# A graph product in seven block products, spread over four bursts of a batch, with k and v moved to the batch's end

## The chip, the cores and the metric

The kernel runs on one core of one Trainium2 chip. The metric is the time of one execution on the device in microseconds (us); lower is better. Engines are named as the profile names them: PE is TensorE (its weight loads apart as PEld), DVE is VectorE, ACT is ScalarE, POOL is GpSimd, SP is SyncE, which here only issues DMAs.

## What is computed

Two graph layers over x of shape (16, 1024, 256), f32. The change lies in the first, which makes its queries from a product with a weighted graph (g below) and then does attention with four heads of 64:

```python
fea = transpose(x, (0, 2, 1))                     # (b, 256, 1024)
c_adj = mean(fea, axis=1)
diff = c_adj[:, None, :] - c_adj[:, :, None]
A = abs(abs(sigmoid(diff) - 0.5) - 0.5) * 2.0
A_s = (A + transpose(A, (0, 2, 1))) * 0.5
Wg = adj[None] * A_s                              # (b, 1024, 1024)
g = relu(einsum('bcn,bnm->bcm', fea, Wg) * para)
q = heads(transpose(g, (0, 2, 1)))
k, v = heads(x @ kv_w)
out = softmax(q @ k.T * scale) @ v
x = layernorm(x + out)
# second layer: A_hat @ x, two linear layers with batch norms, residual, layernorm
```

## The kernel before

The kernel has two paths; `fast_path` is what runs (the other is taken if a denominator leaves its range). It goes through three stages: attention for all 16 batches, then aggregation and the first linear layer, then the second linear layer and the final normalisation. The change touches the first.

**Tiles.** A batch's x is a tile of 128 partitions x 8 chunks x 256 (three buffers, pool xp). Its transpose is xT (one buffer, pool xTp). The weighted graph is eight tiles wg of 128x1024, one for each chunk of rows (pool wgp, eight buffers, so the next batch's weights take the buffers as the graph product frees them). q, k and v of a batch are SBUF tiles with two buffers. PSUM has three pools: s (two tiles of 128x1024, for scores), t (two of 128x512, for everything short: transposes, k, v, graph product, denominators) and o (two of 128x512, the attention outputs).

**Order.** PE, ACT and DVE run in the order in which the code records the instructions (`manual_schedule`); each engine is a queue. POOL and SP instructions start when their inputs and buffers are there and the one ahead in their queue is done. The main loop goes over bursts. A batch has 32 units (2 pairs of heads x 2 halves of queries x 8 chunks of keys), a burst is 2 units, so a batch has 16 bursts, u = 0 to 15. In burst u the code records: the scores of its two units and the exps of them on ACT (`scores`); the outputs of the two units of the burst before and, on DVE, the addition of the exps to acc (`outputs`, L931 and L933); then extra work that u selects. The exps p have four buffers, so the exps of a burst wait for the acc additions of the burst two before.

**Extra work, before.** Denominators (`normalise`): after the last burst of a head pair, in bursts 8 and 0 of the next, four matmuls of acc with ones (den), an ACT copy, four DMAs to DRAM and four back. `residual`: four bursts later (12 and 4), per half of queries a reciprocal, four transposes, a product on DVE and an addition to x on POOL (L979). `finish_x1`: in burst 5, statistics and normalisation on DVE (`layernorm`), then a DMA on POOL's queue that stores x; the next x is loaded into the freed buffer.

For the next batch: bursts 10 and 12 transpose x, with the row means (`begin`) ahead of the first; the means go to DRAM and come back as crow, a row on all partitions. Weights (abs and tanh on ACT, a product with adj on DVE, L793) run in bursts 13 to 15 and 0 to 4. k and v (eight steps) run in bursts 0 and 4. The graph product runs in bursts 6, 8, 10 and 12: 32 matmuls of 128x128 by 128x512 in four groups of eight, each group in one t tile, followed by a product with para and the negative scale on DVE and a relu on ACT (`queries`). In the profile each f32 matmul stands as two records, so 960 records at L805 are 480 matmuls in 15 batches. Batch 0 does its own graph product chunk by chunk before the loop (`graph_first`), with k and v of batches 0 and 1 around it.

**Elsewhere.** `left_sums` and `right_sums` (L658 to L669) and `products` (L604) are the seven-product scheme that the second stage already uses.

Of the kernel before, what the change touches and what calls it, by code (L numbers as in the profile page):

```python
# [515 lines left out]
def fast_path(  # L516
# [74 lines left out]
    def layernorm(t, name):  # L591
        st = small.tile([P, NCH, 6], F32, tag="ln_st", name=f"st_{name}")
        mv = small.tile([P, NCH, 2], F32, tag="ln_mv", name=f"mv_{name}")
        rstd = small.tile([P, NCH], F32, tag="ln_rs", name=f"rs_{name}")
        for n in range(NCH):
            nc.vector.bn_stats(st[:, n, :], t[:, n, :])
            nc.vector.bn_aggr(mv[:, n, :], st[:, n, :])
        rsqrt(rstd, mv[:, :, 1], EPS)
        for n in range(NCH):
            nc.vector.tensor_scalar(  # L600
                t[:, n, :], t[:, n, :], mv[:, n, 0:1], rstd[:, n : n + 1], ALU.subtract, ALU.mult
            )

# [96 lines left out]
    with (  # L700
        tc.tile_pool(name="l0c", bufs=1) as l0c,
        tc.tile_pool(name="qkv", bufs=2) as qkv,
# [30 lines left out]
        def prologue(b):  # L733


            s = st[b]
            xt = s["x"]
            first, steps, side = [], [], []

            def step(f, *a):  # L740
                steps.append((f, a))
# [16 lines left out]
            def transpose_x(c, half):  # L758
                if c == 0 and half == 0 and b:
                    begin()  # L760
# [7 lines left out]
                nc.vector.tensor_copy(s["xT"][:, c, half * HALF : (half + 1) * HALF], pt)  # L768
# [28 lines left out]
            def graph_mm(c, half, part):  # L797
                if part == 0:
                    s["pg"] = tile_t(f"pg_{b}_{c}_{half}")
                    if c == 0 and half == 0:  # L800
                        s["qT"] = qkv.tile([P, CC, N], F32, tag="qT", name=f"qT_{b}")
                ps = s["pg"]
                hs = slice(half * HALF, (half + 1) * HALF)
                for n in (2 * part, 2 * part + 1):
                    nc.tensor.matmul(  # L805
                        ps, xt[:, n, c * P : (c + 1) * P], s["wg", n][:, hs],
                        start=(n == 0), stop=(n == NCH - 1),
                    )
                if part == 3:
                    queries(c, hs, ps)  # L810

            def queries(c, hs, ps):
                q = s["qT"][:, c, hs]
                nc.vector.scalar_tensor_tensor(  # L814
                    q, ps, -scale, para_s[:, c, hs], op0=ALU.mult, op1=ALU.mult
                )
                nc.scalar.activation(q, q, AF.Relu)  # L817

            def graph_first(n):

                if n == 0:
                    both = tile_s("pg_0_0")
                    s["pg"] = [both[:, H0], both[:, H1], tile_o("pg_0_1_0"), tile_o("pg_0_1_1")]
                    s["qT"] = qkv.tile([P, CC, N], F32, tag="qT", name="qT_0")
# [6 lines left out]
                if n == NCH - 1:  # L831
                    for c in range(CC):
                        for half, hs in enumerate((H0, H1)):
                            queries(c, hs, s["pg"][2 * c + half])

            def keys(kc, half):
                if kc == 0 and half == 0:
                    s["kT"] = qkv.tile([P, CC, N], F32, tag="kT", name=f"kT_{b}")
# [7 lines left out]
                nc.scalar.copy(s["kT"][:, kc, hs], ps)  # L846

            def values(pair):
                if pair == 0:
                    s["v"] = qkv.tile([P, NCH, C], F32, tag="v", name=f"v_{b}")  # L850
                pt = tile_t(f"pv_{b}_{pair}")
                for j in range(2):
# [6 lines left out]
                nc.vector.tensor_copy(  # L859
                    s["v"][:, 2 * pair : 2 * pair + 2, :].rearrange("p n c -> p (n c)"), pt  # L860
                )

            for i in range(2 * CC):
                first.append((transpose_x, (i // 2, i % 2) if b else (i % 2, i // 2)))
            if b == 0:
                first += [(begin, ()), (row_of_means, ())]
            for i in range(4):
                step(values, i)
                step(keys, i // 2, i % 2)
            for c in range(CC):  # L870
                for half in range(2):
                    for part in range(4):
                        if b:
                            step(graph_mm, c, half, part)
            for n in range(NCH if b == 0 else 0):
                step(graph_first, n)
            for n in range(NCH):
                side.append((weights_abs, (n,)))
                side.append((weights_tanh, (n,)))
                if n:  # L880
                    side.append((weights_adj, (n - 1,)))
            side.append((weights_adj, (NCH - 1,)))
            return first, steps, side
# [11 lines left out]
        def scores(i):  # L895
            b, pr, qh, m = units[i]
            qT, kT = st[b]["qT"], st[b]["kT"]
            ps = tile_s(f"ps_{i}")
            for kh in range(2):
                for hd in range(2):  # L900
# [3 lines left out]
                        ps[kh * D : (kh + 1) * D, hd * HALF : (hd + 1) * HALF], kT[r, pr, ks],  # L904
                        qT[r, pr, qh * HALF : (qh + 1) * HALF], start=True, stop=True,
# [34 lines left out]
        def normalise(b, pr):  # L940
# [10 lines left out]
            row = rdp.tile([P, HALF], F32, tag="drow", name=f"drow_{k}")  # L951
# [28 lines left out]

        def finish_x1(b):
            xt = st.pop(b)["x"]
            layernorm(xt, f"l0_{b}")
# [602 lines left out]
```

## Time and profile before

| | |
|---|---|
| median of 3 runs | 2651.31 us (2650.74 to 2654.38) |
| the profiled execution | 2653.06 us, span in the profile 2651.3 us |
| mean granted PE clock | 0.981 |
| graph product, L805 | 425.2 us busy in 960 records |
| scores, L903, and outputs, L924 | 490.6 and 485.3 us busy |
| k, L842, and v, L855 | 120.3 and 124.0 us busy |
| exps, L908 (ACT) | 495.7 us busy in 512, 1020 ns each |
| acc, L933 and L931 (DVE) | 483.2 and 78.0 us busy |

A busy time is the time in which at least one instruction of the group ran, so a long group of overlapping matmuls counts once. The mean of one instruction goes from its start to its end; successive instructions on ACT and DVE overlap by about 0.1 us, so the distance between starts is the better price in a sum. The span is from the first to the last instruction of the profiled execution; the execution's own time has 1.8 us around it.

### The profile page before, as it was taken

Reading aid. Unit: us, or ns where it says so; the run is one execution under the profiler, and the core shown is the slowest. Engines: PE = TensorE matmul, PEld = TensorE weight load, DVE = VectorE, ACT = ScalarE, POOL = GpSimd, SP = SyncE. Lnnn points to the kernel's source line nnn. Section 1 sums busy time; section 2 is a strip of 40 time slices with the busy share of each in tenths; the row PEclk is TensorE's granted clock in tenths of the full one; section 3 lists DMA queues with packets and bytes.
Section 4 is the critical chain, followed back from the end, with each engine's and each line's share of the span. In section 5 each row is a group of like instructions: output and inputs, shape, how many; then the busy total and the mean of one; then the engine's idle time right before and its main releaser. Section 6 shows DMA issues by size and latency. Waiting matters only on the chain. (4 is left out here: it accounts for less than half of the span.)

```text
span 2651.3 us, 31994 instructions
## 1 busy us (share of the span) xinstructions
PE 2553.7 (96%) x12966; PEld 1110.1 (42%) x12966; DVE 1600.2 (60%) x2160; ACT 1126.8 (43%) x1349; POOL 336.2 (13%) x407
## 2 busy tenths in 40 slices
PE   8999999999999999999999999999999999999964
PEld 4443444444434434444444343344444444444443
DVE  5465665756656657666566576765655655533376
ACT  5363563654645636545446354410101001233368
POOL 0001000100100011001000100321222211100044
PEclk9999999999999999999999999999999999999975
DMA  4001101001011011010110110112122122353367
GB/s 143 2 9 41 33 10 41 21 22 33 9 41 33 9 41 33 10 41 3 39 33 9 41 49 1 41 64 95 80 95 95 66 92 82 137 202 143 149 222 240
DMA packets 134557, 168.94 MB, mean 64 GB/s; under 512 B 86785, under 2 KB 120065, under 8 KB 124033
## 3 DMA queue, kind: packets, MB, share of 16 engines
q1 hardware_dynamic: 129568, 116.47, 14.2%
q0 software_dynamic: 4832, 50.34, 4.6%
q8 instruction: 103, 1.69, 0.3%
q14 instruction: 54, 0.43, 0.0%
HBM read 99.36 MB, written 67.44 MB: 63 GB/s over the span
## 5 line engine op out<-in xcount | busy, mean ns | idle before, releaser
L908 ACT ACTIVATE p<-ps 128x1024 f32<-128x1024 f32 x512 | 495.7, 1020 | 179.5 <-PE ps L903 142.9
L933 DVE TENSOR_TENSOR acc<-acc,p 128x1024 f32<-128x1024 f32 x384 | 483.2, 1258 | 61.0 <-ACT p L908 32.4
L903 PE MATMUL ps<-qT,kT 64*64 64x512 f32 x4096 | 490.6, 594 | 1.4 <-ACT p L908 1.4
L924 PE MATMUL po<-p,v 64*64 64x512 f32 x4096 | 485.3, 589 | 0.0
L805 PE MATMUL pg<-wg,x 128*128 128x512 f32 x960 | 425.2, 596 | 0.0
L979 POOL TENSOR_TENSOR x<-x,o 128x512 f32<-128x512 f32 x64 | 109.5, 1711 | 1434.8 <-DVE o L974 1434.8
L924 PEld LDWEIGHTS po<-p,v 64*64 64x64 f32 x4096 | 156.7, 133 | 282.8 <-issue 282.6
L805 PEld LDWEIGHTS pg<-wg,x 128*128 128x128 f32 x960 | 177.6, 190 | 226.9 <-issue 203.3
L903 PEld LDWEIGHTS ps<-qT,kT 64*64 64x64 f32 x4096 | 146.1, 132 | 280.2 <-issue 231.5
L817 ACT ACTIVATE qT<-qT 128x512 f32<-128x512 f32 x64 | 40.3, 631 | 482.0 <-DVE qT L814 481.9
L1456 PE MATMUL po<-hl,w12T 128*128 128x512 f32 x512 | 220.3, 592 | 3.1 <-ACT hl L1387 2.3
L814 DVE SCALAR_TENSOR_TENSOR qT<-pg,para_s 128x512 f32<-128x512 f32 x64 | 43.9, 689 | 271.1 <-PE pg L805 269.8
L793 DVE SCALAR_TENSOR_TENSOR wg<-wg,adj_s 128x1024 f32<-128x1024 f32 x128 | 153.1, 1217 | 15.5 <-ACT wg L789 15.5
L784 ACT ACTIVATE wg<-crow,ccol 128x1024 f32<-128x1024 f32 x128 | 146.6, 1146 | 11.8 <-DMA crow<-c 11.8
L1456 PEld LDWEIGHTS po<-hl,w12T 128*128 128x128 f32 x512 | 97.1, 190 | 126.3 <-issue 120.5
L789 ACT ACTIVATE wg<-wg 128x1024 f32<-128x1024 f32 x128 | 135.5, 1060 | 2.6
L1387 ACT ACTIVATE hl<-hl,bn_sh,bn_sg 128x1024 f32<-128x1024 f32 x64 | 74.3, 1229 | 135.0 <-DMA hl<-h 133.6
L855 PE MATMUL pv<-kvw_s,xT 128*128 128x256 f32 x512 | 124.0, 385 | 1.6 <-ACT kT L846 1.6
L1460 DVE TENSOR_SCALAR o<-po,col_b 128x1024 f32<-128x1024 f32 x32 | 41.1, 1284 | 139.1 <-PE po L1456 139.1
L842 PE MATMUL pk<-xT,kvw_s 128*128 128x512 f32 x256 | 120.3, 592 | 0.0
L855 PEld LDWEIGHTS pv<-kvw_s,xT 128*128 128x128 f32 x512 | 94.9, 190 | 51.9 <-issue 27.6
L1286 PE MATMUL a_agg<-ahT,x1l 128*128 128x512 f32 x240 | 108.1, 593 | 1.1 <-ACT agg L1104 1.1
(151 smaller groups left out, 2625.4 us busy)
## 6 DMA issues: line engine op xcount, KB each, us to landing
h<-hw POOLq DMA_DIRECT2D x16, 2048.0 KB, 6.6
hl<-h SPq DMA_DIRECT2D x15, 2048.0 KB
x<-x POOLq DMA_DIRECT2D x16, 1024.0 KB, 4.2
x1l<-x SPq DMA_DIRECT2D x16, 1024.0 KB
xf<-x SPq DMA_DIRECT2D x16, 1024.0 KB
out_dram<-o SPq DMA_DIRECT2D x16, 1024.0 KB
x<-in_x_dram SPq DMA_DIRECT2D x15, 1024.0 KB
crow<-c SPq DMA_DIRECT2D x15, 512.0 KB
```

The source lines that it names most:

```text
L784: nc.scalar.activation(w, s["crow"], AF.Abs, bias=s["ccol"][:, n : n + 1])
L789: nc.scalar.activation(w, w, AF.Tanh, scale=0.5)
L793: nc.vector.scalar_tensor_tensor(w, w, 1.0, adj_s[:, n, :], op0=ALU.subtract, op1=ALU.mult)
L805: nc.tensor.matmul(ps, xt[:, n, c * P : (c + 1) * P], s["wg", n][:, hs], start=(n == 0), stop=(n == NCH - 1),)
L842: nc.tensor.matmul(ps, kvw_s[:, c, kc * P : (kc + 1) * P], s["xT"][:, c, hs], start=(c == 0), stop=(c == CC - 1),)
L855: nc.tensor.matmul(pt[:, j * C : (j + 1) * C], s["xT"][:, c, n * P : (n + 1) * P], kvw_s[:, c, C : 2 * C], start=(c == 0), stop=(c == CC - 1),
L903: nc.tensor.matmul(ps[kh * D : (kh + 1) * D, hd * HALF : (hd + 1) * HALF], kT[r, pr, ks], qT[r, pr, qh * HALF : (qh + 1) * HALF], start=Tr ...
L908: nc.scalar.activation(p, ps, AF.Exp)
L924: nc.tensor.matmul(g["po"][kh][hd * D : (hd + 1) * D, :], s["v"][r, m, h * D : (h + 1) * D], p[r, hd * HALF : (hd + 1) * HALF], start=(m = ...
L933: nc.vector.tensor_add(g["acc"], g["acc"], p)
L979: nc.gpsimd.tensor_tensor(xs, xs, o.rearrange("p n h d -> p n (h d)"), ALU.add)
L1456: nc.tensor.matmul(ps[:, hs], w2T[:, k, c * P : (c + 1) * P], h[k][:, hs], start=(k == 0), stop=(k == HC - 1),)
```

## The change

The graph product of batches 1 to 15 is done as a 2x2 block product in seven block products of four matmuls each (28 matmuls instead of 32), each in a t tile of its own. It needs four sums of blocks of x (`left`, on POOL, in the buffer that xT has) and four differences of blocks of wg (`right_first` to `right_fourth`, 16 DVE subtractions of 128x512; two in new tiles t1 and t2, two in place in wg). The products are put together in q by DVE additions out of PSUM, multiplied with para on POOL, and scaled inside the relu.

The order of a batch's bursts changes with it. The next batch's weights run in bursts 11 to 15 and 0, the differences in 0 to 3 and 5 to 7, the block products in bursts 4 (one), 6, 8 and 10 (two each), the transposes of x at the end of 10, and k and v in bursts 12 and 14, after the graph product. `begin` moves to burst 8. Some copies of xT and v go from DVE to ACT, and the layer norm's application goes from DVE to ACT (`statistics_x1` in burst 4, `finish_x1` in burst 5). The residual of the second head pair moves from burst 4 to 3. q and k get a tile per head pair (three buffers each), the denominator row shares a buffer with o, the weights of the second stage are loaded in burst 1 of the last batch instead of burst 6 of the one before, and the statistics tiles of the batch norms move to other pools.

```diff
     def layernorm(t, name):
+        nmr = small.tile([P, NCH], F32, tag="ln_nm", name=f"nm_{name}")
+        def statistics():
             for n in range(NCH):
                 nc.vector.bn_stats(st[:, n, :], t[:, n, :])
                 nc.vector.bn_aggr(mv[:, n, :], st[:, n, :])
             rsqrt(rstd, mv[:, :, 1], EPS)
+            nc.gpsimd.tensor_tensor(nmr, mv[:, :, 0], rstd, ALU.mult)
+            nc.gpsimd.tensor_scalar(nmr, nmr, -1.0, None, ALU.mult)
-        for n in range(NCH):
-            nc.vector.tensor_scalar(
-                t[:, n, :], t[:, n, :], mv[:, n, 0:1], rstd[:, n : n + 1], ALU.subtract, ALU.mult
+        def apply(n):
+            nc.scalar.activation(
+                t[:, n, :], t[:, n, :], AF.Identity,
+                bias=nmr[:, n : n + 1], scale=rstd[:, n : n + 1],
             )
...
             def transpose_x(c, half):
...
+                copy = nc.scalar.copy if half and b else nc.vector.tensor_copy
...
+            LOW = NCH // 2
+            def right_first(i):
...
+                nc.vector.tensor_sub(S["t1"][:, i, :], w[:, H1], w[:, H0])
+            def right_second(i):
+                nc.vector.tensor_sub(S["t2"][:, i, :], s["wg", i + LOW][:, H1], S["t1"][:, i, :])
+            def right_third(i):
+                w = s["wg", i][:, H1]
+                nc.vector.tensor_sub(w, s["wg", i + LOW][:, H1], w)
+            def right_fourth(i):
+                nc.vector.tensor_sub(
+                    s["wg", i][:, H0], s["wg", i + LOW][:, H0], S["t2"][:, i, :]
+                )
+            def left(k):
+                if k == 0:
+                    S["l"] = xTp.tile([P, 4, LOW, P], F32, tag="xT", name=f"xS_{b}")
...
+                nc.gpsimd.tensor_tensor(l[k], one, two, op)
+            def product(k):
+                ps = tile_t(f"pg_{b}_{k}")
+                w = [s["wg", i] for i in range(NCH)]
+                for i in range(LOW):
...
+                        1: lambda: (xt[:, i, C0], w[i][:, H0]),
+                        2: lambda: (xt[:, i + LOW, C0], w[i + LOW][:, H0]),
+                        3: lambda: (S["l"][:, 3, i, :], w[i + LOW][:, H1]),
+                        4: lambda: (xt[:, i + LOW, C1], w[i][:, H0]),
+                        5: lambda: (S["l"][:, 0, i, :], S["t1"][:, i, :]),
+                        6: lambda: (S["l"][:, 1, i, :], S["t2"][:, i, :]),
+                        7: lambda: (S["l"][:, 2, i, :], w[i][:, H1]),
...
+                    nc.tensor.matmul(ps, one, two, start=(i == 0), stop=(i == LOW - 1))
...
+            def times_para(c, half):
...
+                nc.gpsimd.tensor_tensor(q, q, para_s[:, c, hs], ALU.mult)
+            def graph(k):
...
+                if k == 1:
+                    nc.scalar.copy(a, ps)
+                if k == 6:
+                    nc.vector.tensor_add(u, ps, a)
+                if k == 2:
+                    nc.vector.tensor_add(a, ps, a)
+                    times_para(0, 0)
...
+                if k == 7:
+                    nc.vector.tensor_add(v, ps, u)
+                if k == 4:
+                    nc.vector.tensor_add(low, ps, v)
+                    times_para(1, 0)
+                if k == 5:
+                    nc.vector.tensor_add(u, ps, u)
+                    nc.vector.tensor_add(v, ps, v)
+                    times_para(1, 1)
+                if k == 3:
+                    nc.vector.tensor_add(u, ps, u)
+                    times_para(0, 1)
+            def query_last(c, half):
...
+                nc.scalar.activation(q, q, AF.Relu, scale=-scale)
...
             def values(pair):
...
+                copy = nc.scalar.copy if pair % 2 and b else nc.vector.tensor_copy
...
+                "kv": [
+                    (values, (0,)), (keys, (0, 0)), (values, (1,)), (keys, (0, 1)),
+                    (values, (2,)), (values, (3,)), (keys, (1, 0)), (keys, (1, 1)),
+                ],
+                "graph": [(graph, (k,)) for k in (1, 6, 2, 7, 4, 5, 3)],
+                "relu": [(query_last, q) for q in ((0, 0), (1, 0), (1, 1), (0, 1))],
...
+            for i in range(LOW):
+                for n in (i, i + LOW):
+                    side += [(weights_abs, (n,)), (weights_tanh, (n,)), (weights_adj, (n,))]
+                todo["sums"] += [(f, (i,)) for f in (right_first, right_second)]
+            todo["sums"] += [(f, (i,)) for f in (right_third, right_fourth) for i in range(LOW)]
...
-            row = rdp.tile([P, HALF], F32, tag="drow", name=f"drow_{k}")
+            row = rdp.tile([P, HALF], F32, tag="o", name=f"drow_{k}")
...
+                    wait = 5 if j == len(bursts) - 1 or pr == 0 else 4
                     for q in range(2):
-                        full.setdefault(j + 5, []).append((residual, (b, pr, q)))
+                        full.setdefault(j + wait, []).append((residual, (b, pr, q)))
                     if pr == PAIRS - 1:
+                        late.setdefault(j + 5, []).append((statistics_x1, (b,)))
                         late.setdefault(j + 6, []).append((finish_x1, (b,)))
...
+                todo = nxt if b + 1 < B else {}
+                if u == 0 or u == 1:
+                    part("left", 2)
+                part("side", {0: 3, 1: 99}.get(u, 0))
+                part("sums", {0: 2, 1: 2, 2: 2, 3: 2, 5: 4}.get(u, 0))
+                if u == 4:
+                    part("graph", 1)
+                elif u == 6:
+                    part("graph", 2)
+                    part("sums", 2)
+                elif u == 7:
+                    part("relu", 1)
+                    part("sums", 2)
+                elif u == 8:
+                    run(after.get("begin", []), 1)
+                    part("graph", 2)
+                elif u == 10:
+                    part("graph", 2)
+                    part("xT", 4)
+                elif u == 11:
+                    part("relu", 3)
+                if u in (12, 14):
+                    for i in range(4):
+                        part("kv", 1)
+                        run(after["side"], 1 + i % 2)
+                elif u > 10:
+                    run(after["side"], 3)
+                run(full.get(j, []), 9)
...
                 run(sums.get(j, []), 9)
```

In the loop, `nxt` is the batch after the one whose attention runs and `after` the one behind it: the weights of `after` start in burst 11, and at the next burst 0 `after` becomes `nxt`. What burst u's line `run(sums.get(j, []), 9)` records is `normalise`, the last thing of the burst.

## The prediction

> **What bounds the kernel now.** I read the page's first two parts, then the windows through the attention stage (roughly 75 to 1708 us), then the timelines of the engines over one batch (800 to 912 us).
>
> ```profile
> PE 2553.7 (96%) x12966; PEld 1110.1 (42%) x12966; DVE 1600.2 (60%) x2160; ACT 1126.8 (43%) x1349; POOL 336.2 (13%) x407
> ...
> 460.00:560.00 100.00, 99.41 (x648) 41.49 (x650) 64.01 (x85) 52.53 (x60) 9.42 (x7) 1.00 0.09 23
> ...
> L805 PE MATMUL pg<-wg,x 128*128 128x512 f32 x960 | 425.2, 596 | 0.0
> ```
>
> The second line is one stretch of the windows: length, then busy time of PE, weight loads, DVE, ACT and POOL, and the granted clock. TensorE works 99.4 us of every 100 at full clock; DVE is busy 64, ACT 53, POOL 9. Any matmul removed is time gained, as long as no wait replaces it. TensorE has next to none: two of 0.24 and 0.35 us in a batch. A batch takes 104.9 us (the denominator sums of two batches start at 802.43 and 907.33). Why there are no waits is seen where a batch hands over to the next (start, length, engine, line, operation, count):
>
> ```profile
> 895.50 1.92 ACT L908 ACTIVATE p<-ps 128x1024 f32<-128x1024 f32 x2
> ...
> 897.08 2.55 DVE L933 TENSOR_TENSOR acc<-acc,p 128x1024 f32<-128x1024 f32 x2
> ...
> 898.42 1.90 PE L924 MATMUL po<-p,v 64*64 64x512 f32 x16
> 900.25 1.99 PE L855 MATMUL pv<-kvw_s,xT 128*128 128x256 f32 x8
> 902.08 1.88 PE L842 MATMUL pk<-xT,kvw_s 128*128 128x512 f32 x4
> 903.79 1.89 PE L855 MATMUL pv<-kvw_s,xT 128*128 128x256 f32 x8
> 905.52 1.88 PE L842 MATMUL pk<-xT,kvw_s 128*128 128x512 f32 x4
> 907.33 1.07 PE L946 MATMUL den<-acc,ones 128*32 128x512 f32 x8
> ```
>
> den needs the two acc additions of burst 15. They end at 899.6; TensorE reaches den at 907.3, because 7.1 us of k and v stand ahead of it. Last, DVE beside POOL:
>
> ```profile
> 888.61 1.22 DVE L931 TENSOR_TENSOR acc<-p,p 128x1024 f32<-128x1024 f32 x1
> 889.93 2.12 DVE L933 TENSOR_TENSOR acc<-acc,p 128x1024 f32<-128x1024 f32 x1
> ...
> 888.77 2.19 POOL L979 TENSOR_TENSOR x<-x,o 128x512 f32<-128x512 f32 x1 [0.81 <-DVE o L974]
> ...
> 1893.85 1.70 POOL L661 TENSOR_TENSOR x1S<-x1l 128x512 f32<-128x512 f32 x1
> ...
> 1894.47 1.64 DVE L667 TENSOR_TENSOR tT<-agg,tT 128x512 f32<-128x512 f32 x1
> ```
>
> The POOL addition, 1.26 us alone, takes 2.19 beside an acc; the next acc takes 2.12 instead of 1.22. They take turns, a whole instruction each.
>
> [...]
>
> **The change part by part.** Times between starts: eight f32 matmuls 6.87 us (862.43 to 869.30), a burst of two units 3.43, a k or v step 1.75, exp pair 1.82, abs+tanh 2.16 (0.96 the tanh), ACT copy 0.5, adj 1.13, acc 1.23, 128x512 DVE operation 0.61 to 0.69, POOL 128x512 alone 1.26.
>
> *Removed.* 28 matmuls in place of 32, for 15 batches: 4 x 0.859 x 15 = 51.5 us of TensorE.
>
> *Added work, per batch.* DVE: 16 subtractions and 3 operations more on products, 19 x 0.69 = 13.1; away go 4 copies (2.8) and 8 normalisations (8 x 0.407 = 3.3); +7.0. ACT: 5 copies and 8 normalisations, 5 x 0.58 + 8 x 0.504 (row L1526, the same form) = +6.9. POOL: 4 left sums, 4 products with para, 8 x 1.26 = +10.1. Totals (about 71, 60, 19 of 100) fit; these cost nothing by their sums, only by their places.
>
> *den without cover (the main term).* Burst 0 now has no k and v; TensorE goes from outputs straight to den. The weights of the next batch run from burst 11: two in each of bursts 12 and 14, one in 11, 13, 15, 0. Count from TensorE's start of burst 15, which is the end of the last k step of burst 14. ACT: copies that k to 0.6, then tanh (weight 6) to 1.55, exp pair to 3.4, abs and tanh (weight 3) to 5.55. DVE in order: adj of weight 6 from 1.75 to 2.9, two acc of burst 14 to 5.35, adj of weight 3 from 5.65 to 6.8, two acc of burst 15 to 9.3. TensorE: two bursts to 6.9, the half of den that needs only the older acc to 7.45, then waits to 9.4: 2.0 us, bare. But the left sums write the tile that xT had, so POOL may start them when the last k step ends, at 0.15, not in burst 0 where they stand. Four in a row: the first ends at 1.4, the second at 2.65; adj of weight 6 waits 0.9 for it; the third and fourth go in between the next DVE operations, 1.25 each. adj to 3.75, acc of burst 14 to 6.1 and, after the fourth sum, 8.5, adj 9.65, acc 10.85 and 12.05. den waits from 7.45 to 12.1: 4.65 us. Lower bound 2.0 (no contention), none if DVE were 2 us earlier; upper bound 5 (all four sums delay it). I take 4.65. Batches 1 to 14 have it (15 has no weights behind it): 65 us.
>
> *Bursts 0 to 5.* Behind that wait DVE is 2.45 us behind TensorE as burst 1 starts. It gets 2.5 in burst 1 (one acc, two subtractions), 3.8 in 2, 6.7 in 3 (with the residual's wait for POOL), 3.6 and the statistics 4.3 in 4, each against 3.43 plus what TensorE has there (1.2 in burst 3, 3.5 in 4). Statistics end 5.7 into burst 5; POOL's small ones take 2.8; ACT normalises (4.1, queued ahead of burst 6's exps) to 9.15 into burst 6, exps to 11.0. TensorE needs the second at 11.3, after two products. So 0, with 0.3 to spare; 1.5 per batch if a term is off. The first product's buffer is free at 5.9 into burst 3, needed at 8.1: 0. The x store takes 3.7 and the load 4.7 us (838.9 to 847.2): x is there by 6 into burst 8; its row sums (2.6 us) end before the product that DVE must add for den at 10.5: 0. SP's den stores stand behind crow there, 10.6 us later than before; the residual comes 20 us later: 0.
>
> *Two short waits of TensorE.* Burst 10: the four transposes of x follow the products and use two buffers; the second waits for the DVE addition of the last product, the others for copies: 0.65 x 15 = 10. Burst 14: the third step needs the buffer of the first, whose DVE copy stands behind adj, residual and two acc, to 7.65 after 7.0: 0.65 x 14 = 9. The old 0.35 goes: 15 x 0.35 = -5.
>
> *The rest.* The relus wait for POOL's products with para, but the scores that read them come in the next batch: 0. The denominator row shares a buffer with o, whose readers ended five bursts before: 0. The weights' load in the last batch, six bursts earlier and needed in burst 10, and the moved statistics tiles: 0.
>
> *Ends.* At the start 14 us of k, v move from ahead of burst 0 into its bursts 12 and 14, no gain; but they covered ACT, which gets crow at 42.9 and then has 6 weights (2.13 each) ahead of the first relu; the first scores wait about 2.6 and the second 4.3, against 1.9 + 1.6 that go: +4 with odds and ends. The last batch: about +1 (normalisation ahead of exps, residual earlier).
>
> **Sum.** -51.5 + 65 + 10 + 9 - 5 + 5 = +32.5. The profiled execution took 2653.06 us (span 2651.3 and 1.8 around it), the median is 2651.31, 0.07% less; I apply the sum to the median: 2684 us, 1.2% slower.
>
> **Rivals.** (1) *Only the bare wait.* The left sums end before DVE's stretch or don't block it: 14 x 2.0 = 28 instead of 65, 2647 us. For: POOL's start is inferred from a buffer, not seen. Against: both fences show the turns. (2) *Faster: den's wait hidden.* If DVE ends the acc of burst 15 within 7.45 us of that burst's start, den doesn't wait; it decides at 7.45, against my 9.3 and 12.05. It would happen if ACT did the tanh before the copy of k, or ran further ahead. Then -51.5 + 10 + 9 - 5 + 5: 2619. Against: the queue's order and the durations above; only an error of 2 us in that chain gives it. (3) *More waits.* The 0.3 us in burst 6 is missed, by 1.5 us in 14 batches: +21, 2705. For: six terms in a row, any contention by the products with para on top. Against: the same lateness of TensorE at den gives the others time. That the products are not done as said has no support: they are 28 in the instruction order.
>
> **How the numbers follow.** Likeliest 0.50 (own range 2668 to 2698), rival 1 0.18, rival 2 0.14, rival 3 0.18. About 0.2%, 5.3 us, can be told from no change. Rival 1 straddles that bound: 0.09 faster, 0.05 same, 0.04 slower. Faster 0.09 + 0.13 = 0.22, same 0.05 + 0.02 = 0.07, slower 0.71. The range 2638 to 2712 leaves out most of rival 2 and the far end of rival 3.
>
> **What would show it.** TensorE's busy time falls by about 50 us, yet the span grows; den's matmuls wait for acc some 4 to 5 us, 14 times; left-sum records of 1.3 us and of 2.2 to 2.5; acc or adj beside them 2.1 and more; short waits at the x transposes and the third k, v step of burst 14. Wrong if den waits under 2 us, if the left sums start later than burst 15, or if scores of burst 7 wait for exps.

## The result, and the profile after

The changed kernel takes 2741.64 us (2741.13 to 2743.74, 4 runs) against 2652.85 (2650.74 to 2655.2, 4 runs) of the kernel before: 3.4% slower, ratio 1.0336, 95% interval 1.0318 to 1.0354. The forecast was 2684, range 2638 to 2712: the sign is right, the size is not, and the time lies outside the range. The spans are 2739.3 and 2651.3 us, the mean granted clock 0.968 and 0.981.

The page of the kernel after, its totals and its row of acc (busy us, mean ns of one | idle time ahead):

```profile
PE 2566.2 (94%) x12846; PEld 1087.5 (40%) x12846; DVE 1777.2 (65%) x2257; ACT 1238.6 (45%) x1552; POOL 558.9 (20%) x559
...
L1034 DVE TENSOR_TENSOR acc<-acc,p 128x1024 f32<-128x1024 f32 x384 | 512.8, 1335 | 35.2 <-ACT p L1009 16.3
```

There are 120 matmul records fewer, yet TensorE's busy time is 12.5 us more: some of its matmuls got slower. An acc takes 1335 ns on the mean, 1258 before. The waits of TensorE in the kernel after (us in total, times, longest):

```profile
PE den L1047 <- DVE acc L1034: 52.4, 14, 3.8
...
PE pv L947 <- DVE v L952: 13.2, 14, 0.9
PE pah L1153 <- ACT ahT L1156: 8.5, 4, 7.5
PE pxT L771 <- DVE q L903: 5.2, 15, 0.3
```

den waits for acc 14 times, once in each of the batches for which it was predicted. This is the place in TensorE's timeline (start, length, operation, the wait ahead of it in brackets):

```profile
829.04 1.90 PE L1025 MATMUL po<-p,v 64*64 64x512 f32 x16
830.87 1.05 PE L1047 MATMUL den<-acc,ones 128*32 128x512 f32 x4
835.66 1.92 PE L1047 MATMUL den<-acc,ones 128*32 128x512 f32 x4 [3.75 <-DVE acc L1034]
837.51 3.69 PE L1004 MATMUL ps<-q,k 64*64 64x512 f32 x16
840.98 2.04 PE L1025 MATMUL po<-p,v 64*64 64x512 f32 x16
842.85 1.89 PE L1004 MATMUL ps<-q,k 64*64 64x512 f32 x16
```

Read the starts. The second half of den starts 4.8 us after the first, where 0.5 would do. Then it takes 1.85 us to the next start, and the 16 score records last 3.69; the next 16 score records of the same form last 1.89. Something other than the wait makes the matmuls behind it slow. The windows over the same stretch show what (length, then busy time and instructions of PE, weight loads, DVE, ACT and POOL, the granted clock, DMA share, GB/s):

```profile
832.00:834.00 2.00, 0.00 (x0) 0.00 (x0) 2.00 (x3) 1.83 (x3) 0.00 (x0) 1.00 0.00 0
834.00:836.00 2.00, 0.34 (x2) 0.19 (x4) 1.97 (x3) 1.78 (x2) 0.00 (x0) 0.61 0.00 0
836.00:838.00 2.00, 2.00 (x8) 0.31 (x8) 1.97 (x4) 0.33 (x1) 0.00 (x0) 0.50 0.00 0
838.00:840.00 2.00, 2.00 (x12) 0.50 (x8) 2.00 (x3) 0.69 (x2) 0.00 (x0) 0.50 0.04 12
840.00:842.00 2.00, 2.00 (x20) 0.65 (x15) 1.97 (x3) 1.32 (x2) 0.00 (x0) 0.68 0.29 6
842.00:844.00 2.00, 2.00 (x24) 0.70 (x20) 1.90 (x3) 0.34 (x2) 0.00 (x0) 1.00 0.27 2
```

The granted clock falls to half within the pause and stays there until about 841. The whole-run mean, 0.968 against 0.981, hides this: it is 7 us in one batch and 3.4 in the next.

The cause of the wait is as predicted. DVE and POOL in the same stretch of the kernel after:

```profile
825.52 2.12 DVE L800 SCALAR_TENSOR_TENSOR wg<-wg,adj_s 128x1024 f32<-128x1024 f32 x1 [2.68 <-ACT wg L796]
827.57 4.51 DVE L1034 TENSOR_TENSOR acc<-acc,p 128x1024 f32<-128x1024 f32 x2
832.00 1.21 DVE L800 SCALAR_TENSOR_TENSOR wg<-wg,adj_s 128x1024 f32<-128x1024 f32 x1
833.14 2.47 DVE L1034 TENSOR_TENSOR acc<-acc,p 128x1024 f32<-128x1024 f32 x2
```

```profile
824.05 2.52 POOL L837 TENSOR_TENSOR xS<-x 128x512 f32<-128x512 f32 x2 [7.97 <-ACT wg L791]
826.50 2.28 POOL L837 TENSOR_TENSOR xS<-xS,x 128x512 f32<-128x512 f32 x1
828.86 2.13 POOL L837 TENSOR_TENSOR xS<-x,xS 128x512 f32<-128x512 f32 x1
```

The four left sums (the first line has two) start at 824.05, 0.14 us behind the last matmul of burst 14's last k step, though they are recorded in bursts 0 and 1. While they run, the adj product takes 2.12 us and two acc 4.51; without them, from 832.0 on, 1.21 and 2.47. That is 0.9 + 2.0 us, and the last acc ends at 835.6.

To see where the 88 us went, I took two batches of each kernel in TensorE's timeline (802.43 to 1012.23 before, 830.87 to 1052.73 after), and summed the time from each start to the next by kind. A wait is then counted with the kind ahead of it, for den with den's own first half. Per batch:

| kind | before, us | after, us | difference |
|---|---|---|---|
| graph product | 27.88 | 24.73 | -3.15 |
| den | 1.99 | 7.65 | +5.66 |
| scores | 27.76 | 29.08 | +1.32 |
| k and v | 14.07 | 15.75 | +1.68 |
| outputs, transposes of x and o | 33.20 | 33.72 | +0.52 |
| a batch | 104.9 | 110.93 | +6.03 |

From den of burst 8 in batch 0 to den of burst 8 in batch 14 the kernel after takes 83.2 us longer, a little less than 14 times 6.03. Ahead of that the start is 9.2 us shorter (110.4, before 119.6), and from there to den of burst 8 in the last batch it is 16.2 longer: +7.0 together. The two belong together, since the k and v of one batch moved from the start into batch 14, and they contain the graph product of the 15th batch. What follows takes 2.2 less: 88.0, as the spans say.

### The profile page after: what moved, and what is told of

Its sections match the earlier page's. It is cut to its first block, busy times and chain, and to the rows that moved or that the text cites. A ratio compares the mean times of both kernels' runs of the same rounds, so it can differ in the third digit from the quotient of the medians.

```text
span 2739.3 us, 32218 instructions
## 1 busy us (share of the span) xinstructions
PE 2566.2 (94%) x12846; PEld 1087.5 (40%) x12846; DVE 1777.2 (65%) x2257; ACT 1238.6 (45%) x1552; POOL 558.9 (20%) x559
## 5 line engine op out<-in xcount | busy, mean ns | idle before, releaser
L1034 DVE TENSOR_TENSOR acc<-acc,p 128x1024 f32<-128x1024 f32 x384 | 512.8, 1335 | 35.2 <-ACT p L1009 16.3
L1004 PE MATMUL ps<-q,k 64*64 64x512 f32 x4096 | 512.0, 617 | 2.7 <-ACT p L1009 2.7
L800 DVE SCALAR_TENSOR_TENSOR wg<-wg,adj_s 128x1024 f32<-128x1024 f32 x128 | 184.7, 1446 | 201.3 <-ACT wg L796 201.3
L1004 PEld LDWEIGHTS ps<-q,k 64*64 64x64 f32 x4096 | 146.9, 137 | 306.8 <-issue 274.9
L872 POOL TENSOR_TENSOR q<-q,para_s 128x512 f32<-128x512 f32 x60 | 81.7, 1361 | 432.2 <-DVE q L896 186.6
L852 PE MATMUL pg<-wg,x 128*128 128x512 f32 x360 | 163.4, 596 | 0.0
L852 PE MATMUL pg<-t,xS 128*128 128x512 f32 x240 | 111.0, 605 | 0.0
L1047 PE MATMUL den<-acc,ones 128*32 128x512 f32 x256 | 60.0, 698 | 52.8 <-DVE acc L1034 52.4
L852 PE MATMUL pg<-wg,xS 128*128 128x512 f32 x240 | 109.4, 599 | 0.0
```

Source lines behind the costliest of these rows:

```text
L800: nc.vector.scalar_tensor_tensor(w, w, 1.0, adj_s[:, n, :], op0=ALU.subtract, op1=ALU.mult)
L852: nc.tensor.matmul(ps, one, two, start=(i == 0), stop=(i == LOW - 1))
L1004: nc.tensor.matmul(ps[kh * D : (kh + 1) * D, hd * HALF : (hd + 1) * HALF], kT[r, ks], qT[r, qh * HALF : (qh + 1) * HALF], start=True, stop ...
L1034: nc.vector.tensor_add(g["acc"], g["acc"], p)
```

## Experiments

What was open: whether the slow clock is really what the prediction lacked, how much of it is the contention of the left sums, and whether den's missing cover can be had without loss elsewhere. All times are medians of at least 4 runs; the kernel before took 2653.6 to 2654.8 us on the same chips. "Period" is the distance between two batches' den in the trace: before 104.9, after 110.4 and 111.5 in turn.

**Useless matmuls in the pause.** Four matmuls of adj into den's own tile, which den then overwrites:

```diff
             den = tile_t(f"den_{k}")
+            if pr == PAIRS - 1 and b < B - 2:
+                for i in range(4):
+                    nc.tensor.matmul(den, adj_s[:, i, C0], adj_s[:, i, H0], start=True, stop=True)
```

> Ahead of den in the 14 batches concerned, four matmuls of 128x512 without use (blocks of adj, 3.4 us) keep TensorE at work in the time in which it would wait; DVE, ACT and POOL are unchanged. It adds 56 matmuls, 48 us of TensorE. Theory A (part of the loss is the clock that is granted after the pause): den's second half ends when it did, the clock stays at 1.00, the stretch of den, scores and outputs goes, 14 x 2.8 = 39 us gained, about 2702 us. Rival (the matmuls after den are slow for another reason, such as reading what DVE has just written): no gain, 2742 us or more.

Measured 2719.16 us, ratio 1.0244 (1.0227 to 1.0261). TensorE's timeline with the four:

```profile
822.17 3.70 PE L1048 MATMUL den<-adj_s 128*128 128x512 f32 x8
825.80 2.20 PE L1052 MATMUL den<-acc,ones 128*32 128x512 f32 x8
827.93 1.95 PE L1004 MATMUL ps<-q,k 64*64 64x512 f32 x16
```

48 us of work that nobody needs were added, and the kernel became 22.5 us faster. acc still sets the end of den; what went is the slow clock: the granted clock is 1.00 from 67 to 1725 us, and the scores behind den take 1.77 us to the next start again. The period is 109.14, in two batches 109.5. This shows the cause; the size is smaller than the expected 2.8 us a batch. Bursts 0 and 1 take 2.2 us less on the mean of the changed kernel's two kinds of batch; the expectation had taken the batch shown above, with 7 us at half clock, for all of them, while in every second one, with 3.4, the same scores take 2.5 us instead of 3.47. And 0.4 went again in burst 7, as a later run explains.

**The left sums late.** Two edits: POOL into the recorded order, and all four left sums in burst 3 behind the residual.

```diff
-        with tc.manual_schedule(engines={mybir.EngineType.PE, mybir.EngineType.Activation, mybir.EngineType.DVE}):
+        with tc.manual_schedule(engines={mybir.EngineType.PE, mybir.EngineType.Activation, mybir.EngineType.DVE, mybir.EngineType.Pool}):
...
-                if u == 0 or u == 1:
-                    part("left", 2)
...
+                if u == 3:
+                    part("left", 4)
```

> The four left sums on POOL are recorded in burst 3 behind the residual's additions, and POOL keeps the recorded order, so none runs beside bursts 15 and 0; den stays uncovered. Theory A1 [...]: den's second half waits about 2 us less than in the changed kernel, 1 to 2 us in place of 3.75; if that is too short for the clock to drop, 14 x 5.5 = 77 us are gained, about 2665 us; if the clock still drops, 14 x 2.7 = 38 us, about 2704 us. Rival A2 (POOL has no part, the queue of DVE and ACT alone makes the wait): wait 3.75 us as before, 2742 us.

Measured 2688.57 us, ratio 1.0129 (1.0112 to 1.0146), 53 us less than the changed kernel, period 107.0. The DVE and the TensorE timeline of this run:

```profile
806.34 2.48 DVE L1034 TENSOR_TENSOR acc<-acc,p 128x1024 f32<-128x1024 f32 x2
809.15 1.23 DVE L800 SCALAR_TENSOR_TENSOR wg<-wg,adj_s 128x1024 f32<-128x1024 f32 x1 [0.33 <-ACT wg L796]
810.29 2.48 DVE L1034 TENSOR_TENSOR acc<-acc,p 128x1024 f32<-128x1024 f32 x2
```

```profile
810.54 1.05 PE L1047 MATMUL den<-acc,ones 128*32 128x512 f32 x4
812.83 1.05 PE L1047 MATMUL den<-acc,ones 128*32 128x512 f32 x4 [1.23 <-DVE acc L1034]
813.81 1.95 PE L1004 MATMUL ps<-q,k 64*64 64x512 f32 x16
```

No acc and no adj product is stretched, the wait falls from 3.75 to 1.23 us, and the clock stays at 1.00. The contention made two thirds of the wait, and through the wait all of the slow clock at den. Where 5.5 us a batch were expected (2665 us), bursts 0 and 1 take 4.7 us less, and 0.8 went again in burst 7, whose scores now wait 0.65 us for exps. Here one also sees what a listed wait of 1.23 us costs: den takes 3.27 us from start to next start where 1.0 is usual. The list counts from the end of the last matmul. Each half of den lasts 1.05 us to the end of its last matmul, but where no wait follows the next work starts after 0.5; here it starts after 1.05 and the wait, and after 0.98 behind the second half. So TensorE loses about 1 us more than the list says.

**k and v of burst 14 back in burst 0, ahead of den.** Once as they were, once with the k step first in each pair:

```diff
+                cover = []
                 if u == 0 and b:
+                    cover = nxt["kv"]
                     nxt, after = after, {"side": []}
...
+                run(cover, 4)
...
-                        part("kv", 1)
+                        if u == 12:
+                            part("kv", 1)
```

> The four k and v steps of burst 14 are recorded in burst 0, ahead of den, as before the change; all else as changed. Theory A (the uncovered den wait costs 7.5 us in each of 14 batches: 3.75 us of waiting inside den, 0.9 us by which den's second half is stretched, 1.7 and 0.15 us by which the scores and outputs after it are stretched at half the granted clock, and about 1 us of restart): no den wait over 0.3 us, granted clock 1.00 through the attention stage, 2741.6 - 14 x 7.5 = about 2637 us. Rival B (DVE and POOL carry too much altogether, and den is only the first place where it shows): the wait moves into bursts 1 to 7 (scores waiting for exps), at least 3 us a batch, time over 2690 us.

> As the run with k and v in burst 0, and the steps of bursts 12 and 0 alternate k first, then v, so that the third step needs a PSUM buffer that ACT empties and not one that waits in DVE's queue. Expected: the wait of 0.94 us of the third step in burst 12 goes, 15 x 1 = 15 us less than that run, about 2622 us, which is 1.2% faster than the kernel before. Rival: the wait only moves to the fourth step, no difference between the two runs.

Measured 2764.05 us (ratio 1.0416, 1.0399 to 1.0433) and 2732.99 (1.0301, 1.0284 to 1.0319). den no longer waits for acc in either, but the 2637 and 2622 us of theory A are far off: rival B was right in kind, and the first is slower than the changed kernel. Now the scores wait for exps, as the second kernel's list of waits of TensorE says:

```profile
PE ps L1004 <- ACT p L1009: 81.0, 46, 2.4
```

Without k and v in burst 14 TensorE has nothing to do beside ACT's weights of that burst, so the scores of burst 0 wait 2.36 us for exps; those of burst 3 wait 1.65 and those of burst 7 1.55. As the burst stands, the four steps can cover one place or the other: ACT's weights or den. With the k step first the wait for v in burst 12 is gone, and a batch takes 109.63 us instead of 111.62 where the clock stays at full in both. The two kernels have the same wait at the same place, and yet TensorE's timeline differs behind it, first without, then with the k step first:

```profile
832.33 2.94 PE L1004 MATMUL ps<-q,k 64*64 64x512 f32 x16 [2.36 <-ACT p L1009]
835.03 2.66 PE L1025 MATMUL po<-p,v 64*64 64x512 f32 x16
```

```profile
818.34 2.00 PE L1004 MATMUL ps<-q,k 64*64 64x512 f32 x16 [2.36 <-ACT p L1009]
820.16 1.90 PE L1025 MATMUL po<-p,v 64*64 64x512 f32 x16
```

A pause of 2.36 us halved the clock here in the first and not in the second. Over the whole stage it is 10 of the 14 pauses in the first and 4 of 14 in the second. So the length of the pause alone doesn't decide.

**A shorter pause, and a shifted one.** First one useless matmul instead of four:

> The changed kernel with one useless matmul of adj (0.86 us) ahead of den where the run with four had them, so that TensorE pauses 3.4 us instead of 4.3 (from the issue of the last matmul of the first half). The end of den is set by acc and doesn't move. Theory A, the clock is halved by one pause longer than some limit: the limit lies between the 1.8 us of the late left sums, where it stayed at 1.00, and 4.3 us; if 3.4 us is still over it, the time stays at 2742 +- 4 and the granted clock shows 0.5 in each batch; if it is under it, 2719 as with four, clock 1.00. Rival B, the loss grows with the length of the pause without a limit: in between, about 2735, each batch stretched a little less.

Measured 2725.29 us, ratio 1.0268 (1.0251 to 1.0285), period 109.14. Two of its pauses at den, of the same length, in the middle and at the end of the stage:

```profile
827.05 1.05 PE L1052 MATMUL den<-acc,ones 128*32 128x512 f32 x4 [2.68 <-DVE acc L1034]
828.03 1.95 PE L1004 MATMUL ps<-q,k 64*64 64x512 f32 x16
...
1591.08 1.92 PE L1052 MATMUL den<-acc,ones 128*32 128x512 f32 x4 [2.69 <-DVE acc L1034]
1592.94 3.69 PE L1004 MATMUL ps<-q,k 64*64 64x512 f32 x16
```

In 13 of the 14 pauses the clock stays at full, in the last one it is halved. (That pause makes 2.6 of the 6 us by which this run is above the one with four; of the 4.7 us that its span is longer, 3.0 lie behind the attention stage.) By the 13 alone one would write down "2.7 us are harmless".

But the trace's record of the granted clock has a regularity: in every run its changes lie on points 3.413 us apart (to within 0.005 us in the traces of the kernels before and after). I summed TensorE's idle time, as listed, for each such stretch of the attention stage in all traces. Where the clock was at full, 1.89 us of idle time or less left the next stretch at full, and 1.97 or more put it at half; in the kernel after alone the two figures are 1.29 and 2.10. (Behind that stage there are exceptions in the kernel before: 1.72 and 1.88, and then half.) In the run with one matmul the period is 31.98 stretches, so from batch to batch the border moves by only 0.08 us against the pause. The larger side of the cut pause is 1.76 us in the first batch, falls to 1.36, rises again by 0.08 a batch to 1.89 in the 13th, and is 1.97 in the last, the one that halves the clock.

To test this, two more useless matmuls, half a batch away, where nothing waits:

```diff
-            if pr == PAIRS - 1 and b < B - 2:
-                for i in range(1):
+            if b < B - 2:
+                for i in range(1 if pr == PAIRS - 1 else 2):
```

> The run with one useless matmul ahead of the last den of a batch, and two more useless matmuls (1.7 us) ahead of the den of burst 8, where TensorE waits for nothing, half a batch away from the pause. The trace's record of the granted clock changes only at points 3.413 us apart, in every run; in the traces so far the clock is halved for the next such window wherever TensorE was idle for 2.0 us or more of one, and never at 1.89 or less. In the run with one useless matmul the batch takes 109.14 us, 31.98 windows, so every pause of 2.7 us is cut by a window's border in the same way (1.5 to 1.9 us on one side) and escapes. Theory A, the phase decides: 1.72 us more is half a window, the pauses now fall inside a window in at least every second batch and the clock halves there although the pause is no longer: 2725 + 14 x 1.72 = 2749 and 1.5 us for each halved batch, 2760 to 2773. Rival B, only the length of the pause decides: none is halved, 2749.

Measured 2756.78 us, ratio 1.0389 (1.0373 to 1.0405). The timeline of TensorE at one of its pauses, which is no longer than before:

```profile
1176.60 1.05 PE L1052 MATMUL den<-acc,ones 128*32 128x512 f32 x4
1180.33 1.91 PE L1052 MATMUL den<-acc,ones 128*32 128x512 f32 x4 [2.68 <-DVE acc L1034]
1182.17 2.73 PE L1004 MATMUL ps<-q,k 64*64 64x512 f32 x16
```

11 of the 14 pauses now halve the clock; the three that don't have 1.58, 1.72 and 1.89 us on the larger side. The phase is part of the cause, as theory A said, though its 2760 to 2773 us were a little high. It also explains the turns in the changed kernel: two of its batches are 221.86 us, 65.0 stretches, so the pause of 3.75 us in turn fills one whole stretch (one stretch at half clock follows, 3.4 us) and lies over a border, 2.53 us on one side and 1.22 on the other (two at half clock, 6.8 us).

**den one scores pair later.**

```diff
                 for i in bursts[j]:
                     scores(i)
+                run(sums.get(j - 1, []), 9)
...
-                run(sums.get(j, []), 9)
```

> The changed kernel with den recorded one scores pair later (after the scores of the next burst). The scores of burst 1 need the PSUM tiles that the exps of burst 0 read, which end at 831.0 and 833.2 in the changed kernel's trace, beside den's first half at 830.9; so TensorE's one pause of 4.3 us breaks into several of at most 1.5 us, den still ends with acc at 836.1, and 1.7 us of scores are done by then. Theory A (single long pause halves the clock): no halved clock; per batch 840.98 - 836.6 = 4.4 us less, 14 batches, 2680 us. Rival B (idle time summed over some stretch halves the clock, not one pause): only the 1.7 us of cover is gained, 2718 us, clock 0.5 still seen around den.

Measured 2720.87 us, ratio 1.0249 (1.0232 to 1.0266). The clock stays at 1.00, as A said, but the time is that of rival B. TensorE's timeline:

```profile
824.68 1.09 PE L1004 MATMUL ps<-q,k 64*64 64x512 f32 x8 [1.12 <-ACT p L1009]
825.70 1.05 PE L1047 MATMUL den<-acc,ones 128*32 128x512 f32 x4
827.10 1.05 PE L1047 MATMUL den<-acc,ones 128*32 128x512 f32 x4 [0.34 <-DVE acc L1034]
...
861.20 2.00 PE L1004 MATMUL ps<-q,k 64*64 64x512 f32 x16 [1.55 <-ACT p L1009]
```

From the start of burst 15's outputs (820.47) to the start of burst 0's (828.08) it now takes 7.6 us instead of the 11.9 of the batch shown above. Bursts 0 and 1 together take 3.9 us less on the mean, but the period falls by 1.6 only. 2.0 us are taken back in burst 7: its scores wait 1.55 us for exps that stand on ACT behind the layer norm's application. ACT waits there for POOL's small operations and these for the statistics on DVE; that DVE is late from the same acc is read from the queues, not tested apart. In the changed kernel the first of these exps ends at 871.26 and the scores start at 872.15. This margin of 0.9 us is used up as soon as TensorE is earlier by more (a wait of 0.24 us in the runs with useless matmuls).

**The small waits, then den later, then the layer norm.** Three kernels, each on top of the one before. The first has the left sums late (two in burst 3, two in 5), k first, the transposes of x in burst 11 instead of 10, and in the last batch the adj transposes of burst 6 in burst 7. The second adds den later. The third adds:

```diff
-                        late.setdefault(j + 6, []).append((finish_x1, (b,)))
+                        late.setdefault(j + 7, []).append((finish_x1, (b,)))
...
-                if u == 5 and b + 2 < B:
+                if u == 6 and b + 2 < B:
...
                 elif u == 8:
-                    run(after.get("begin", []), 1)
                     part("graph", 2)
+                elif u == 9:
+                    run(after.get("begin", []), 1)
```

> The changed kernel with the left sums late (two in burst 3, two in burst 5, POOL in recorded order), k first in the k and v steps, the transposes of x one burst later (11), and in the last batch the transposes of adj of burst 6 moved to burst 7. Against the run with the left sums in burst 3 (2688.6): the waits for v (0.94 and 0.20), for the xT buffer (0.35), for exps in burst 7 (0.65) and the 7.5 us wait for ahT with the halved clock behind it (3 us) should go. Theory A, each of these is TensorE time: 14 x 1.79 + 15 x 0.35 + 10 = 40, 2648 us, den's wait 1.2 as before. Rival B, DVE and ACT are late anyway and the waits come back at den or at the scores: 2675 or more.

> The run with the small waits removed, and den recorded after the scores of the next burst as well. There acc of burst 15 ends about 1.8 us after den's first half could start, and the scores of burst 1 take 1.72 us. Theory A: den no longer waits, 2.27 us less in each of 14 batches, 32 us less than the run without this, about 2616 us, faster than before by 1.4%. Rival B: the scores of burst 1 wait for the exps of burst 0 (ends at 810.95 in the run with the left sums in burst 3, needed at 810.5), and den's copy on ACT comes behind the exps, so that the wait only changes its name: within 10 us of the run without it.

> The run with den later and the small waits removed, and also the layer norm's application recorded after the exps of burst 6 instead of ahead of them (the x store, the load of the next x and the row means one burst later with it). In that run the scores of burst 7 wait 1.56 us in each batch for exps that stand behind the normalisation on ACT (833.5 to 837.5), and 7.0 us with a halved clock behind it in the last batch. Theory A, this is TensorE time: 14 x 1.56 and some 9 us in the last batch, 31 us less, about 2645 us. Rival B, the next x comes later, and its row means and the products' additions behind them on DVE make TensorE wait in bursts 8 to 10: 2665 or more.

Measured 2683.45 us (1.0106, 1.0089 to 1.0123), 2675.66 (1.0078, 1.0061 to 1.0095) and 2653.06 (0.9995, 0.9987 to 1.0003). In the first two rival B was right: against the run with the left sums in burst 3 the first brought 5 us, not 40, and den later another 8, not 32. The waits changed their names: den in burst 8 of the first now waits 0.54 us for a product's addition (0.90 twice, 1.5 once), the second x transpose waits 0.42 in both (1.5 once), the scores of burst 7 wait 0.56 in the first and 1.56 in the second, and in the last batch 7.0 instead of the adj transposes. ACT in the second, ahead of those scores:

```profile
833.49 4.04 ACT L607 ACTIVATE x<-x,nm_l,rs_l 128x256 f32<-128x256 f32 x8 [8.25 <-POOL nm_l L604]
837.43 1.91 ACT L1009 ACTIVATE p<-ps 128x1024 f32<-128x1024 f32 x2
```

ACT stands idle 8.25 us with exps behind the normalisation in its queue. With the normalisation behind those exps this wait is gone in all batches, and the third kernel is level with the kernel before: 22.6 us less than the second, of the 31 of theory A.

**The last two.** The x transposes ahead of the outputs in burst 11, so that their copies go ahead of acc on DVE; and then the last batch's adj transposes in burst 5.

```diff
+                if u == 11 and b + 1 < B:
+                    run(nxt["xT"], 4)
                 if j:
                     back(j - 1)
```

> The same, and also the transposes of x recorded ahead of the outputs in burst 11, so that DVE copies them ahead of the acc additions (they wait 1.5 us in every second batch when recorded behind them, and 0.35 us in burst 10). Theory A: 7 us less than without this, about 2638 us. Rival B: the copies delay acc of burst 10, exps and outputs move with them, and nothing is gained.

> The fastest version so far (layer norm applied after the exps of burst 6, transposes of x ahead of the outputs), with the last batch's transposes of adj of burst 7 moved to burst 5, ahead of the normalisation on ACT: there they waited 6.0 us for ahT, once, with a halved clock of 6.8 us behind it. Theory A: 6.0 + 3 less, about 2635 us. Rival B: ACT's exps are late in turn and the wait comes back at the scores of burst 7 or 8, within 3 us of the version without this.

Measured 2643.66 us, ratio 0.9963 (0.9949 to 0.9976), 9.4 us less than the kernel without, where 7 were expected, and 2640.34, ratio 0.9947 (0.9933 to 0.996). The last is faster than both kernels, by 0.5% and 3.7%; the 0.5% is small but clear of the noise. The gain of the first does not lie where it was expected: the second x transpose still waits 0.42 us in every batch, as before (the 1.5 stood in one batch only); it is burst 12, with k and v, that takes 0.6 us less a batch. TensorE's timeline of the last one:

```profile
736.62 1.06 PE L1047 MATMUL den<-acc,ones 128*32 128x512 f32 x8
...
790.98 1.62 PE L1047 MATMUL den<-acc,ones 128*32 128x512 f32 x8
...
840.30 1.07 PE L1047 MATMUL den<-acc,ones 128*32 128x512 f32 x8
```

A batch takes 103.7 us and no den waits. The last step brought 3 us of the expected 9, so rival B was nearly right: in the last batch a wait of the scores of 2.9 us came in place of the 6.0 for ahT. Of the 3.0 us that the seven products save in such a batch, 1.2 are left; summed as above, in the version without the last step a den of burst 0 costs 1.55 us instead of 1.0, outputs 0.98 more a batch, scores 0.38 more, and two waits of 0.42 and 0.24 are left.

## Why the prediction was right about the sign and wrong about the size

The sum said +32.5, the spans differ by 88.0. Of the 55.5 us between them, 31 lie in the term of den, 17 in the two short waits, 5 in the ends and 4 in the removed matmuls; 2 come back behind the loop.

- **What bounds the kernel**, TensorE, and that any new wait of it is time: right. But TensorE's busy time, which was to fall by about 50 us, rose by 12.5: matmuls themselves became slower, and no term allowed for that.
- **Removed matmuls**, -51.5: measured 3.15 x 15 = 47. The products come four at a time now, and four followed by something else take 3.53 us, not 3.43.
- **den without cover, the failed step.** The prediction counted "den waits from 7.45 to 12.1: 4.65 us", 65 us in all. The cause of the wait, its place, its count and its bare length are right: from the due start of den's second half (830.87 + 0.5) to its start at 835.66 it is 4.3 us. What the term left out is the state in which TensorE comes out of the wait. The second half of den takes 1.85 us instead of 0.5, and the scores of a batch 1.32 more, because the clock is halved for 3.4 or 6.8 us, some of it inside the pause; about 0.5 of it is the restart, seen at full clock too. Summed over the 14 batches den and scores make +96 us instead of 65: about 60 are the bare wait, 7 the restart, and 30 the slow clock, which the run with four useless matmuls measured apart (2.2 us a batch). The pauses of 3.75 us halved the clock in all 14 batches; shorter ones did it too, 2.36 us in 10 of 14 places of the first run with k and v back in burst 0. The upper bound of 5 us for den was a bound on the wait alone, so the range could not hold the time either.
- **Contention of the left sums** in burst 15: right in cause, time and size; the run with the left sums late shows it. An adj product takes 2.12 us beside a left sum and 1.21 without.
- **Two short waits and the old one**, +14: wrong in size. k, v, outputs and transposes take 2.2 us more a batch, 31 us, of which no run here separates every part. The wait for v lies in burst 12, not 14 (0.94 us, and 0.20 in 14), and each listed wait costs more than its listed length. The x transposes wait 0.35, not 0.65.
- **Bursts 0 to 5, "0, with 0.3 to spare"**: right in the changed kernel, where the margin is 0.9 us, and more important than it looked. This margin is the next bound; it took back 2.0 of the 3.9 us a batch that bursts 0 and 1 gained in the run with den later, and 1.6 of 2.3 in the second run of small waits. Rival 3 is not what happened, but its mechanism is what stands behind den.
- **Ends**, +5: about +10 (the +7.0 above contains the 3.15 that the 15th batch saves). At the start about 4 us came back as waits, as predicted. In the last batch, +1 predicted, the transposes of adj wait 7.46 us for ACT, which stands behind the normalisation, with a halved clock behind it; that wait was not seen.
- **Rivals 1 and 2** assumed that the left sums don't block DVE or that DVE is earlier; neither holds. Without the contention the wait is 1.23 us as listed, and 2.3 us in time, near rival 1's 2.0.

## What to carry to other kernels

A wait of TensorE had three parts here: the wait as listed, about a microsecond of running out and starting again (den took 3.27 us with a listed wait of 1.23, where 1.0 is usual), and the slow clock behind it, which came where about 2 us of the pause (1.97 or more) fell into one stretch of 3.413 us; price all three, and look at the granted clock in windows of 2 us right behind a wait. Work that is moved away from a place may have been the cover of that place, and the cover that it gives elsewhere is not free either: before moving it back, look for the queue entry (here left sums on POOL, a normalisation on ACT ahead of exps) that makes the other engine late. When a wait is removed, the next margin in the batch decides what is gained, so write down the small margins and not only the waits.

## What the runs showed of the hardware

- The granted clock changed on points 3.413 us apart in all 14 traces. In their attention stages, some 7000 stretches, one at full clock with 1.97 us or more of listed idle time was followed by one at half clock, and one with 1.89 or less was not; behind that stage, in the kernel before, 1.72 and 1.88 were followed by half. In the attention stage of the kernel after, a stretch at half clock with 1.15 us or more was followed by another, one with 0.44 or less by full clock. Pauses of 2.36 us (the two runs with k and v back in burst 0) and of 2.68 (the two with one useless matmul at den) were enough where they fell well within one stretch, and escaped where a border cut them.
- So one and the same pause can cost nothing or, as an estimate, up to 1.7 us for each stretch at half clock behind it (half of 3.413), by the length of the loop around it. With a batch of 109.14 us 13 of 14 pauses of 2.68 us escaped; with 221.86 us for two batches the pauses took turns. Adding 1.7 us of matmuls to every batch cost 31 us instead of 24.
- Useless matmuls in a pause can pay: 48 us of them made the kernel 22.5 us faster, since they ran where TensorE stood still and kept the clock at full (1.00 from 67 to 1725 us).
